# Layer-norm statistics of the one-head layers: combined on GpSimd in two parts of four chunks instead of one of eight

## The chip, the cores and the metric

The kernel runs on one core of a Trainium2 chip. The metric is the device time of one execution in microseconds (us), from the first to the last instruction; three executions of the kernel before lay between 2588.01 and 2589.99 us. Four engines compute: TensorE (PE in the profile, with its weight loads as PEld), VectorE (DVE), ScalarE (ACT) and GpSimd (POOL). SyncE (SP) issues the transfers.

## What is computed

The input `x` has 16 graphs of 1024 nodes with 256 features; `adj` is one 1024 x 1024 adjacency matrix for all. Four layers follow one another, and each one adds its result to `x`:

```python
h = jnp.maximum(_layernorm(x, axis=-1), 0.0)   # per node: (x - mean) / sqrt(var + 1e-5)
Wh = h @ W                                     # 256 x 256; 4 heads of 64, or 1 head of 256
e = leaky_relu(e_src[i] + e_dst[j])            # e_src, e_dst: Wh times two vectors
attn = softmax(where(adj, e, -inf), over j)
x = x + act(attn @ Wh)                         # elu in layers 0 to 2, relu in layer 3
```

Layers 0 and 2 have four heads, layers 1 and 3 have one. So there are 16 x 4 = 64 pairs of graph and layer, which the kernel calls steps: 32 of four heads and 32 of one.

## The kernel before

**Tiling.** A graph is held as `xs[b]`, 128 partitions x 8 chunks (`C`) x 256 features; `HALF` is four chunks. For one head, `weights` makes eight tiles of 128 x 1024 un-normalised attention weights on VectorE (`w`, line 347, in 18 buffers), and `aggregate` multiplies them with the projected features on TensorE (line 363). A step's aggregation is written as eight groups: in a four-head step four chunks of 128 nodes for one head, in a one-head step one chunk of nodes. Each group ends in a copy out of a PSUM bank by ScalarE (line 378).

**Order.** Four graphs are in flight (`STREAMS`), and the steps take turns among them, in the main alternating one four-head and one one-head step. The order of all instructions is written out by hand[...]. `preparation(n)` gives the pieces of work that step n needs before its aggregation, and each piece has a place in an agenda, counted in groups (8 to a step). Step n's preparation is spread over the aggregation of step n-2 and a little of n-1. For a one-head step the places are in `ONE`, from the start of step n-2:

```python
ONE = (2, 2, 2, 4, 4, 5, 5, 6, 6, 6, 6, 6, 6, 8, 8, 8, 8, 8, 10, 10, 12)
```

These are, in turn: the statistics of both halves (`stats(0)`, `stats(1)`) and their combination (`combine_all`) behind group 2; `normalise(0)` and `normalise(1)` behind group 4; the two transposes of half 0 behind group 5; the projection of half 0 (four chunks) and the two transposes of half 1 behind group 6; the rest later. The usual four-head step (`FOUR`) has its statistics eight groups before its start and its `combine_all` five before, so its combination comes behind group 3 of the same aggregation in which the next one-head step is prepared, and its `normalise(0)` behind group 5.

**The pieces around the change.**
- `finish` ends a step. Its `add(0)` and `add(1)` add the layer's result to `x`: one operation on VectorE (line 417), then one on GpSimd (line 418), for each half. After a four-head step they stand behind group 1 of the following aggregation, and the `stats` behind group 2 read the `x` that they wrote: a one-head layer of a graph follows its four-head layer at once.
- `stats` takes the eight chunks' statistics on VectorE (line 234), four chunks to a half.
- `combine` and `combine_end` turn them into a factor and a shift per node by ten operations, all on GpSimd for every step but the first: nine small ones, and a power (line 263).
- `normalise` applies them on ScalarE, one operation per chunk (line 275, tile `xn`).
- `transpose` turns four chunks on TensorE into a PSUM bank (line 283); ScalarE takes them out through a relu (line 284, tile `hT`).
- `project` multiplies a chunk with the layer's weights into a bank (line 294), and ScalarE copies it out (line 296, tile `whx`).

The banks are taken in turn by all of these from one pool of four, `ps`:

```python
ps = ctx.enter_context(tc.tile_pool(name="ps", bufs=4, space=PSUM))
```

Of the kernel before, what the change touches and what calls it, by code (L numbers as in the profile page):

```python
# [63 lines left out]
def kernel(ctx: ExitStack, tc: tile.TileContext, x, adj, ws, avs, out):  # L64
    nc = tc.nc
# [3 lines left out]
    HALF = C // 2  # L69
# [152 lines left out]
    def preparation(n):  # L222

        b, l = steps[n]
        H, slope, _, _ = LAYERS[l]
# [3 lines left out]
        def stats(half):  # L229
            if half == 0:  # L230
                st["bn"] = small.tile([P, C, 6], F32, name="bn")
            bn = st["bn"]
            for c in range(half * HALF, (half + 1) * HALF):
                nc.vector.bn_stats(bn[:, c, :], xs[b][:, c, :])  # L234
            if n == 0:
                q = slice(half * HALF, (half + 1) * HALF)
                if half == 1:
                    combine_end(slice(0, HALF), nc.vector)
                combine(q, nc.vector)
                if half == 1:  # L240
                    combine_end(q, nc.vector)

        def combine_all():
            if n > 0:
                combine(slice(0, C), nc.gpsimd)
                combine_end(slice(0, C), nc.gpsimd)

        def combine(q, engine):

            bn = st["bn"]  # L250
            m0, s0, m1, s1 = (bn[:, q, i] for i in (1, 2, 4, 5))
            if q.start == 0:
                st["rstd"] = small.tile([P, C], F32, name="rstd")
                st["shift"] = small.tile([P, C], F32, name="shift")
                st["dev"] = small.tile([P, C], F32, name="dev")
            rstd, shift, dev = (st[i][:, q] for i in ("rstd", "shift", "dev"))
            engine.tensor_tensor(dev, m0, m1, op=ALU.subtract)  # L257
            engine.tensor_tensor(dev, dev, dev, op=ALU.mult)
            engine.tensor_scalar(dev, dev, 0.25, EPS, op0=ALU.mult, op1=ALU.add)
            engine.tensor_tensor(rstd, s0, s1, op=ALU.add)  # L260
            engine.tensor_scalar(rstd, rstd, 1.0 / F, None, op0=ALU.mult)
            engine.tensor_tensor(rstd, rstd, dev, op=ALU.add)
            nc.gpsimd.tensor_tensor(rstd, rstd, neghalf[:, q], op=ALU.pow)  # L263
            engine.tensor_tensor(shift, m0, m1, op=ALU.add)  # L264

        def combine_end(q, engine):
            rstd, shift = (st[i][:, q] for i in ("rstd", "shift"))
            engine.tensor_tensor(shift, shift, rstd, op=ALU.mult)
            engine.tensor_scalar(shift, shift, -0.5, None, op0=ALU.mult)  # L269
# [45 lines left out]
        def rows():  # L315
# [6 lines left out]
            nc.sync.dma_start(out=st["grow"].rearrange("h c i -> c h i"), in_=gT)  # L322

        out = [lambda: stats(0), lambda: stats(1), combine_all, lambda: normalise(0), lambda: normalise(1)]
        for half in range(2):
            out += [lambda half=half, k=k: transpose(half, k) for k in range(K)]
# [130 lines left out]
    def plan(n):  # L457
        new = preparation(n)
        agenda.extend((at, n, piece, i == len(new) - 1) for i, (at, piece) in enumerate(new))
        agenda.sort(key=lambda a: a[:2])  # L460
# [52 lines left out]
    with tc.manual_schedule():  # L513
# [10 lines left out]
        nc.vector.tensor_copy(identb, ident)  # L524
        layer[0][1]()
        first = [piece for _, piece in preparation(0)]

        def sign(c):
# [98 lines left out]
```

## Time and profile before

| what | value |
|---|---|
| time, median of three | 2589.18 us |
| span of the profiled execution | 2586.6 us |
| granted TensorE clock, mean | 0.992 |
| busy: PE, PEld | 2508.0, 2257.8 us |
| busy: DVE, ACT, POOL | 2024.0, 1129.3, 1034.3 us |
| transfers | 128.98 MB, 50 GB/s on average |

A row of a group of instructions names the line, the engine, the operation and the tiles (written <- read), then the busy time, the mean of one in ns, and the idle time of the engine just before them with what ended it. A row of the timeline has the start in us, the length in us, the engine and the instructions, and in brackets the engine's idle time before them. The chain of waits is followed backwards from the last instruction: at each step to what released it, or to the instruction before it on its engine. Matmul ends are modelled, so a stretch in which PE counts as busy can hide a part of a wait; the starts of the weight loads (PEld) are then the better clock.

### The profile page before, as it was taken

How to read it: one execution, taken by the hardware profiler on the slowest of the kernel's cores; microseconds unless marked ns; L12 is line 12 of the kernel's file. 1: busy time of each engine (PE TensorE's matmuls, PEld its weight loads, DVE VectorE, ACT ScalarE, POOL GpSimd, SP SyncE). 2: the span in 40 equal slices, each digit the busy share in tenths (PEclk: the TensorE clock that was granted, in tenths of full speed). 3: DMA queues.
4: the chain of work that ended last, by engine and by line, in shares of the span. 5: the costliest groups of instructions: out<-in, count | busy, mean ns of one | idle time of the engine just before them, and what ended most of it. 6: DMA issues, size and time to landing. Idle time of an engine off the chain costs nothing.

```text
span 2586.6 us, 87821 instructions
## 1 busy us (share of the span) xinstructions
PE 2508.0 (97%) x40088; PEld 2257.8 (87%) x40088; DVE 2024.0 (78%) x2144; ACT 1129.3 (44%) x2502; POOL 1034.3 (40%) x1040
## 2 busy tenths in 40 slices
PE   6889999999999999999999999999999999999999
PEld 4788888899888899888899888998888998889888
DVE  5997678877778877778877778877778877787973
ACT  5344444434444444544344544344444345444341
POOL 2143444432443444543323444543433345444331
PEclk8899999999999999999999999999999999999999
DMA  3210011111112100102211111101112201111101
GB/s 142 73 44 35 18 34 43 43 60 59 59 51 76 43 27 27 43 35 75 76 53 66 43 35 43 43 19 68 50 59 76 76 11 43 35 43 43 52 18 57
DMA packets 36987, 128.98 MB, mean 50 GB/s; under 512 B 6278, under 2 KB 9094, under 8 KB 34696
## 3 DMA queue, kind: packets, MB, share of 16 engines
q1 hardware_dynamic: 36606, 123.36, 13.6%
q8 instruction: 314, 5.14, 0.8%
q14 instruction: 57, 0.47, 0.1%
q10 hardware_dynamic: 10, 0.00, 0.0%
HBM read 105.91 MB, written 17.43 MB: 48 GB/s over the span
## 4 chain that ended last, share of the span: by engine, by line
PE 57%; DVE 26%; POOL 9%; issue 5%; ACT 3%; DMA 1%; DVEq 0%; SPq 0%; ACTq 0%
PE bank L363 36%; DVE w L347 17%; PE bank L294 17%; POOL x L418 5%; PE bank L283 4%; DVE bn L234 3%; DVE e L417 2%; ACT xn L275 2%; DVE e L404 2%; POOL rstd L263 2%; DMA x<-in_x 0%; ACT e L411 0%; PE bank L318 0%; DVE r L395 0%; POOL shift L269 0%
## 5 line engine op out<-in xcount | busy, mean ns | idle before, releaser
L363 PE MATMUL bank<-whx,w 128*64 128x65 f32 x36864 | 1904.8, 241 | 32.6 <-DVE w L347 20.8
L363 PEld LDWEIGHTS bank<-whx,w 128*64 128x64 f32 x36864 | 1742.1, 144 | 176.5 <-DVE w L347 25.5
L347 DVE SCALAR_TENSOR_TENSOR w<-g,rcol,mask 128x1024 f32<-128x1024 f32 x1280 | 1540.4, 1273 | 378.0 <-PE bank L363 337.3
L378 ACT ACTIVATE y<-bank 128x260 f32<-128x260 f32 (+1 forms) x504 | 194.4, 386 | 1093.4 <-PE bank L363 1093.4
L306 POOL TENSOR_TENSOR whx<-whx 128x1024 f32<-128x1024 f32 x128 | 258.5, 2020 | 666.0 <-ACT whx L304 666.0
L405 POOL TENSOR_TENSOR y<-y,r 128x1024 f32<-128x1024 f32 x126 | 264.4, 2108 | 582.1 <-DVE e L404 454.9
L294 PE MATMUL bank<-wx,hT 128*128 128x264 f32 (+1 forms) x2048 | 476.5, 387 | 3.7 <-ACT hT L284 3.7
L294 PEld LDWEIGHTS bank<-wx,hT 128*128 128x128 f32 x2048 | 384.6, 191 | 66.3 <-ACT hT L284 4.6
L418 POOL TENSOR_TENSOR x<-x,e 128x1024 f32<-128x1024 f32 x96 | 248.0, 2593 | 135.7 <-DVE e L417 135.7
L275 ACT ACTIVATE xn<-x,shift,rstd 128x256 f32<-128x256 f32 x512 | 261.2, 590 | 82.9 <-POOL shift L269 80.8
L296 ACT ACTIVATE whx<-bank 128x264 f32<-128x264 f32 (+1 forms) x512 | 194.9, 386 | 208.1 <-PE bank L294 207.7
L234 DVE BATCH_NORM_STATS2 bn<-x 128x6 f32<-128x256 f32 x512 | 175.9, 412 | 97.2 <-POOL x L418 74.0
L417 DVE SCALAR_TENSOR_TENSOR e<-e,y 128x1024 f32<-128x1024 f32 x96 | 158.0, 1663 | 34.2 <-ACT e L411 26.9
L283 PE MATMUL bank<-ident,xn 128*128 128x128 f32 x1024 | 155.2, 281 | 22.9 <-ACT xn L275 22.4
L283 PEld LDWEIGHTS bank<-ident,xn 128*128 128x128 f32 x1024 | 120.4, 141 | 59.6 <-ACT xn L275 48.5
L342 ACT ACTIVATE g<-gs 128x1024 f32<-128x1024 f32 x160 | 163.6, 1022 | 11.1 <-DVE w L347 8.4
L284 ACT ACTIVATE hT<-bank 128x512 f32<-128x512 f32 x256 | 136.6, 585 | 0.3 <-PE bank L283 0.2
L263 POOL TENSOR_TENSOR rstd<-rstd,neghalf 128x8 f32<-128x8 f32 (+1 forms) x65 | 107.0, 1646 | 12.5 <-DVE shift L264 7.6
L411 ACT ACTIVATE e<-e 128x1024 f32<-128x1024 f32 x96 | 100.7, 1049 | 12.7 <-DVE e L404 12.7
L404 DVE SCALAR_TENSOR_TENSOR e<-y,r 128x1024 f32<-128x1024 f32 x64 | 75.6, 1222 | 2.5 <-DVE r L395 0.5
L420 DVE SCALAR_TENSOR_TENSOR x<-y,x 128x1024 f32<-128x1024 f32 x30 | 43.4, 1445 | 10.0 <-POOL y L405 10.0
L257 POOL TENSOR_TENSOR dev<-bn 128x8 f32<-128x8 f32 x63 | 14.6, 231 | 87.4 <-DVE bn L234 87.4
(63 smaller groups left out, 401.7 us busy)
## 6 DMA issues: line engine op xcount, KB each, us to landing
gs<-grow SPq DMA_DIRECT2D x160, 512.0 KB
x<-in_x SPq DMA_DIRECT2D x15, 1024.0 KB
out<-x SPq DMA_DIRECT2D x30, 512.0 KB
w<-in_adj SPq DMA_DIRECT2D x8, 512.0 KB
x<-in_x SPq DMA_DIRECT2D x2, 512.0 KB
wx<-in_L_gnn_W SPq DMA_DIRECT2D x8, 128.0 KB
out<-x SPq DMA_DIRECT2D x8, 128.0 KB
grow<-gT SPq DMA_DIRECT2D x32, 16.0 KB
```

What stands on the lines that cost most here:

```text
L234: nc.vector.bn_stats(bn[:, c, :], xs[b][:, c, :])
L275: nc.scalar.activation(xn[:, q, :], xs[b][:, c, :], AF.Identity, bias=st["shift"][:, c:c + 1], scale=st["rstd"][:, c:c + 1])
L283: nc.tensor.transpose(pt[:, q, :], st["xn", half][:, q, k * P:(k + 1) * P], ident)
L294: nc.tensor.matmul(pw, lhsT=st["hT", half][:, k, q * P:(q + 1) * P], rhs=wx[l][:, k, :], start=(k == 0), stop=(k == K - 1))
L296: nc.scalar.activation(st["whx"][:, c, :], pw, AF.Copy)
L306: nc.gpsimd.tensor_tensor(wh[:, :, :, 0:D], wh[:, :, :, 0:D], wh[:, :, :, D:D + 1].to_broadcast([P, HALF, H, D]), op=ALU.mult)
L347: nc.vector.scalar_tensor_tensor(w, state[n]["g", h], state[n]["rcol"][:, jc, h:h + 1], masks[LAYERS[steps[n][1]][3]][:, jc, :], op0=ALU.m ...
L363: nc.tensor.matmul(acc[o % P:o % P + cols, q, :], lhsT=st["w", h, jc][:, o:o + cols], rhs=st["whx"][:, jc, h * (D + 1):(h + 1) * (D + 1)], ...
L378: nc.scalar.activation(st["y"][:, i0:i0 + per, h, :], acc, AF.Copy)
L405: nc.gpsimd.tensor_tensor(yh, yh, rb, op=ALU.mult)
L417: nc.vector.scalar_tensor_tensor(e, e, -1.0, yh, op0=ALU.add, op1=ALU.max)
L418: nc.gpsimd.tensor_add(xh, xh, e)
```

## The change

In a one-head step, each half's statistics are combined on GpSimd at once behind their own `stats`, four chunks at a time, and `combine_all` is left to the four-head steps. It is for letting the first half's combination start before the second half's statistics are there, and for letting `normalise(0)` start before the second half is combined. The places in the agenda stay as they are.

```diff
             for c in range(half * HALF, (half + 1) * HALF):
                 nc.vector.bn_stats(bn[:, c, :], xs[b][:, c, :])
+            q = slice(half * HALF, (half + 1) * HALF)
             if n == 0:
-                q = slice(half * HALF, (half + 1) * HALF)
                 if half == 1:
                     combine_end(slice(0, HALF), nc.vector)
                 combine(q, nc.vector)
                 if half == 1:
                     combine_end(q, nc.vector)
+            elif H == 1:
+
+                combine(q, nc.gpsimd)
+                combine_end(q, nc.gpsimd)
 
         def combine_all():
-            if n > 0:
+            if n > 0 and H > 1:
                 combine(slice(0, C), nc.gpsimd)
                 combine_end(slice(0, C), nc.gpsimd)
```

## The prediction

> **What bounds the kernel now.** I read the page's busy shares first, then the groups by line with their waits, then the chain of waits in one round of the repeating pattern, and last the timelines of PEld, POOL and ACT around the place where the chain leaves GpSimd.
>
> The busy shares and two groups of the page:
>
> ```profile
> PE 2508.0 (97%) x40088; PEld 2257.8 (87%) x40088; DVE 2024.0 (78%) x2144; ACT 1129.3 (44%) x2502; POOL 1034.3 (40%) x1040
> ...
> L275 ACT ACTIVATE xn<-x,shift,rstd 128x256 f32<-128x256 f32 x512 | 261.2, 590 | 82.9 <-POOL shift L269 80.8
> ...
> L283 PEld LDWEIGHTS bank<-ident,xn 128*128 128x128 f32 x1024 | 120.4, 141 | 59.6 <-ACT xn L275 48.5
> ```
>
> TensorE is close to full. The largest wait of its weight loads is for `xn`, 48.5 us, and `xn` waits for the last operation of the combination. The rest of the question is how much of this is in one-head steps and on the path.
>
> The chain of waits between 1095 and 1180 us, one round of two steps (start, length, what):
>
> ```profile
> 1121.45 5.60 POOL x L418 x2
> ...
> 1128.56 0.22 POOL dev L257
> ...
> 1130.28 1.67 POOL rstd L263
> ...
> 1132.50 0.25 POOL shift L269
> 1132.75 0.02 issue
> 1132.78 2.08 ACT xn L275 x4
> 1134.86 0.04 issue
> 1134.90 0.77 PE bank L283 x5
> ```
>
> The chain comes from VectorE, passes the two adds of `finish`, the second half's statistics, the whole combination and four `xn`, and only then is on PE, where it stays until 1175.0. The weight loads there:
>
> ```profile
> 1115.92 17.24 PEld L363 LDWEIGHTS bank<-whx,w 128*128 128x128 f32 x80
> 1133.43 0.14 PEld L283 LDWEIGHTS bank<-ident,xn 128*128 128x128 f32 x1 [0.26 <-ACT xn L275]
> 1133.92 0.14 PEld L283 LDWEIGHTS bank<-ident,xn 128*128 128x128 f32 x1 [0.35 <-ACT xn L275]
> 1134.41 0.14 PEld L283 LDWEIGHTS bank<-ident,xn 128*128 128x128 f32 x1 [0.35 <-ACT xn L275]
> 1134.90 0.53 PEld L283 LDWEIGHTS bank<-ident,xn 128*128 128x128 f32 x5 [0.35 <-ACT xn L275]
> 1135.40 3.34 PEld L363 LDWEIGHTS bank<-whx,w 128*128 128x128 f32 x16
> 1138.77 3.46 PEld L294 LDWEIGHTS bank<-wx,hT 128*128 128x128 f32 x16
> 1142.26 1.01 PEld L283 LDWEIGHTS bank<-ident,xn 128*128 128x128 f32 x8
> 1143.24 0.74 PEld L363 LDWEIGHTS bank<-whx,w 128*128 128x128 f32 x4
> ```
>
> From 1133.17, when PEld is free, to 1135.40 are 2.23 us. The same eight transposes without a wait take 1.01 us (1142.23 to 1143.24). So this round loses 1.22 us. The wait list of PEld for 1095 to 1173 us has, beside these 1.3 us, only three waits of 0.2 to 0.3 us: nothing else holds TensorE up in a round. I went through all starts of line 283 in this way: from 432 to 2303 us there are 25 such places, about 78 us apart. In 24 of them the transposes are paced by `xn`; before the first of these the wait is 0 in three, 0.19 to 0.27 in thirteen, and 0.62 to 0.72 in eight. One (1290 us) loses only 0.35. Before 432 us the pattern is mostly VectorE's, and behind 2303 us there are small losses at 2359 and one at 2470, where the chain runs on through VectorE.
>
> [...] the combination takes 1128.56 to 1132.71, 4.15 us, when the next one follows at once. [...] the four-head step's combination stands ready from about 1119.3 us (its statistics end there) and starts at 1132.71, behind the other. [...] four `bn_stats` take 1.41 us both beside the second add (1124.76) and beside an idle GpSimd (1127.07). So I charge nothing for running small GpSimd operations beside them.
>
> **The change, part by part.**
>
> Removed: the wait of the first half for the second half's statistics. GpSimd is free at 1127.04, the first half's statistics are there at 1126.17, and the combination starts only at 1128.56. 1.5 us go.
>
> Cost of a part of four. The page groups kept apart by shape give:
>
> ```profile
> L263 POOL TENSOR_TENSOR rstd<-rstd,neghalf 128x8 f32<-128x8 f32 x63 | 105.0, 1666 | 4.9
> L263 POOL TENSOR_TENSOR rstd<-rstd,neghalf 128x4 f32<-128x4 f32 x2 | 2.0, 1024 | 7.6 <-DVE shift L264 7.6
> ```
>
> The power falls from 1.67 to 1.02 us. The nine small ones take about 0.2 us at eight columns; four columns are not in the trace on GpSimd, so between the same and, for scale, VectorE's 0.16. I keep them as they are: 4.15 - 0.64 = 3.51 us a part. Ends: if power and small ones had not shrunk at all, 4.15; if the small ones lost 0.04 each, 3.15.
>
> New times in this round, GpSimd: part one 1127.1 to 1130.6, part two (statistics there at 1128.5) to 1134.1, then the four-head step's combination, 4.15 us, to 1138.3. Before, it ended at 1136.88: it comes 1.4 us later. That is the cost, 2.9 us more of GpSimd in each one-head step (32 x 2.9 = 92 us of a 40% busy engine).
>
> New times, ACT: it is free at 1130.52. `xn` of half 0 from 1130.65 to 1132.7, all before TensorE comes at 1133.2. `xn` of half 1 waits for part two and starts at 1134.15; at the 0.49 us pitch of the trace four take 1.97 us, then the copy of group 5 at 1136.1 (before: 1136.72) and the two `hT` from 1136.4 to 1137.5 (before 1136.99). Queued behind half 1's wait are just these; the copy and `hT` get earlier all the same.
>
> TensorE: transposes at 1133.2, group 6 from 1134.2, projection from 1137.55, 1.22 us earlier, and `hT` is just there (first chunk 1137.0, second 1137.5). The whole wait is gone up to here.
>
> Then the moved combination bites. On ACT the four-head step's `normalise(0)` is next: it started at 1137.94 and now waits for 1138.3. Behind it are the copy of group 6 and those of the projection. Copy of group 6: start 1138.35 + 1.97 = 1140.3, end 1140.7 (before 1139.91, 1140.28). With four banks in turn (group 5, two transposes, group 6, then four chunks of the projection) the projection's fourth chunk needs exactly the bank of group 6. It started at 1138.98 + 3 x 0.87 = 1141.6; 1.22 us earlier is 1140.4; the bank is free at 1140.75. TensorE waits some 0.35 us, and 0.85 us stay. In the rounds with 0.72 us of first wait the transposes gain 1.68, but the bank is tied to GpSimd in the same way (add ends 1205.15, bank free at 1218.85, chunk before at 1219.7): 0.85 again. Where the first wait is 0, the gain of 0.96 is cut to 0.85 too.
>
> Does the gain last? From 1143 to 1175 the chain is on PE without a gap, and at 1175 the end of a group frees `w` buffers, which starts the VectorE chain that leads to the next adds. All of it moves with TensorE. VectorE's own order is unchanged, so the adds do not come later.
>
> Sum: 24 x 0.85 + 0.35 = 20.8 us; the small losses at 147, 273 and 2359 us (0.3 + 0.35 + 0.7) are on the path only in part, I take half, 0.7. Together 21.4 us: 2589.2 - 21.4 = 2567.8 us.
>
> **The rivals.**
> 1. The whole wait goes. If small operations shrink, or the fourth chunk doesn't wait for that bank, the gain is the loss itself: 24 x 0.96 + 8.8 (the sum of the first waits) + 0.4 + 0.7 = 33 us, 2556 us. For it: 0.04 us off each small operation would bring the four-head combination back by 0.7 us. Against it: operations of one column on GpSimd took 190 to 234 ns in this trace, so little depends on width.
> 2. Slower, by GpSimd's queue. If a part of four costs as much as eight (4.15 us), the three end at 1139.6, the copy of group 6 at 1142.0, and the fourth chunk starts 0.45 us later than before: 25 x 0.45 = 11 us, 2600 us. For it: 2.9 us already move a combination that ACT waits for in order. Against it: the power at four columns is in the trace, 1.02 us.
> 3. Slower, by the tracking of dependencies. If `xn` of half 0 waited for both parts, it would start at 1134.15, 1.4 us late: 25 x 1.4 = 35 us, 2624 us. Against it: in the first step, combined by halves already, `xn` starts at 9.23 us while the second power runs at 10.15.
> 4. No change: another chain of the same length takes over, VectorE's `w` for instance. Against it: every VectorE stretch in the round is released by TensorE. 2588 us.
>
> **How the numbers follow.** The forecast has 0.65, the first rival 0.19, the fourth 0.05, the second 0.08, the third 0.03. The predicted time is the forecast's, 2568 us. The range goes from the first rival's bound, 2555, to 2583, where a part costs 3.8 us, leaving 0.3 us a round. Faster by over 0.2% (5.2 us): 0.65 + 0.19 and a little of the uncertain sizes off, 0.83. Same 0.06, slower 0.11.
>
> **What would show it.** Right: the first `dev` (L257) of a round starts within 0.1 us of the end of the second add; the power appears 66 times at four columns, at 1.0 us, and 31 times at eight; the waits of L283 for `xn` fall from 48.5 us to about 10; a wait of L294 for ACT's copy appears at the fourth chunk, about 0.35 us in each round; rounds are 76.8 instead of 77.65 us. Wrong: `xn` of half 0 starting behind both parts; no bank wait at all (then rival 1); L283 waiting at the second half or at the four-head step.

## The result, and the profile after

The changed kernel takes 2569.4 us (median of four, 2568.6 to 2570.3), the kernel before 2588.6 us beside it: a ratio of 0.9927, with a 95% interval of 0.991 to 0.9944. That is 19 us, 0.7%. The forecast was 2568 us, a gain of 21.4 on the 2589.2 us from which it started. (Lines below `stats` have moved down by four: the transposes are L287, the projection L298, the aggregation L367, the copy of a group L382, the copy of `gT` L324.)

The rows of the page after the change that answer to those shown of before, with the one of the projection:

```profile
PE 2496.9 (97%) x40088; PEld 2258.1 (88%) x40088; DVE 2022.6 (79%) x2144; ACT 1129.5 (44%) x2502; POOL 1106.9 (43%) x1360
...
PE 85%; DVE 8%; ACT 3%; issue 2%; POOL 2%; DMA 1%; SPq 0%; DVEq 0%; POOLq 0%; ACTq 0%
...
L298 PEld LDWEIGHTS bank<-wx,hT 128*128 128x128 f32 x2048 | 382.3, 191 | 79.6 <-ACT y L382 14.9
...
L287 PEld LDWEIGHTS bank<-ident,xn 128*128 128x128 f32 x1024 | 120.0, 142 | 24.8 <-ACT xn L279 11.6
```

GpSimd is 73 us busier by its spans, and the kernel is faster. The transposes' wait for `xn` has fallen from 48.5 to 11.6 us. A wait of 14.9 us is new: the projection waits for the copy of a group out of its bank. The chain of waits was 57% on PE and 26% on DVE; it is now 85% and 8%.

The same place of a round as in the prediction, in the timeline of the changed kernel. GpSimd and ScalarE first:

```profile
1112.88 5.59 POOL L422 TENSOR_TENSOR x<-x,e 128x1024 f32<-128x1024 f32 x2 [1.16 <-DVE e L421]
...
1118.42 0.21 POOL L261 TENSOR_TENSOR dev<-bn 128x4 f32<-128x4 f32 x1
...
1121.99 2.08 ACT L279 ACTIVATE xn<-x,shift,rstd 128x256 f32<-128x256 f32 x4
...
1125.48 2.08 ACT L279 ACTIVATE xn<-x,shift,rstd 128x256 f32<-128x256 f32 x4 [1.41 <-POOL shift L273]
...
1129.65 2.07 ACT L279 ACTIVATE xn<-x,shift,rstd 128x256 f32<-128x256 f32 x4 [0.87 <-POOL shift L273]
1131.63 0.36 ACT L382 ACTIVATE y<-bank 128x257 f32<-128x257 f32 x1
```

The combination starts where the second add ends. The three lots of `xn` are those of the first half, of the second half, and of the four-head step; the last two wait for GpSimd. In the kernel before, the first lot began 5.74 us after the end of the second add (1127.04 to 1132.78); now it begins 3.5 us after it. Behind the third lot stands the copy of group 6. The weight loads of TensorE in that place:

```profile
1124.62 1.01 PEld L287 LDWEIGHTS bank<-ident,xn 128*128 128x128 f32 x8
1125.60 3.34 PEld L367 LDWEIGHTS bank<-whx,w 128*128 128x128 f32 x16
1128.97 2.58 PEld L298 LDWEIGHTS bank<-wx,hT 128*128 128x128 f32 x12
1132.05 0.73 PEld L298 LDWEIGHTS bank<-wx,hT 128*128 128x128 f32 x4 [0.49 <-ACT y L382]
```

The eight transposes run in one piece. Then come the projection's first three chunks, and the fourth waits for the copy.

The length of a round of two steps is taken on ScalarE, from one copy of `gT` of a four-head step to the next (`gT` is a small tile that every step writes once; it has 32 rows in a four-head step). First the kernel before, then the changed one:

```profile
1117.35 0.25 ACT L320 ACTIVATE gT<-bank 32x128 f32<-32x128 f32 x1
...
1194.99 0.25 ACT L320 ACTIVATE gT<-bank 32x128 f32<-32x128 f32 x1
```

```profile
1108.78 0.25 ACT L324 ACTIVATE gT<-bank 32x128 f32<-32x128 f32 x1
...
1185.55 0.25 ACT L324 ACTIVATE gT<-bank 32x128 f32<-32x128 f32 x1
```

The round here is 76.77 us, and 77.64 in the kernel before.

### The profile page after: what moved, and what is told of

Its sections match the earlier page's. It is cut to its first block, busy times and chain, and to the rows that moved or that the text cites. A ratio compares the mean times of both kernels' runs of the same rounds, so it can differ in the third digit from the quotient of the medians.

```text
span 2566.8 us, 88141 instructions
## 1 busy us (share of the span) xinstructions
PE 2496.9 (97%) x40088; PEld 2258.1 (88%) x40088; DVE 2022.6 (79%) x2144; ACT 1129.5 (44%) x2502; POOL 1106.9 (43%) x1360
## 4 chain that ended last, share of the span: by engine, by line
PE 85%; DVE 8%; ACT 3%; issue 2%; POOL 2%; DMA 1%; SPq 0%; DVEq 0%; POOLq 0%; ACTq 0%
PE bank L367 65%; PE bank L298 15%; DVE w L351 6%; PE bank L287 4%; ACT xn L279 2%; DVE bn L234 1%; DVE e L421 1%; POOL x L422 0%; POOL rstd L267 0%; DMA x<-in_x 0%; PE bank L322 0%; ACT y L382 0%; POOL shift L273 0%; DVE e L408 0%; DVE wx L156 0%
## 5 line engine op out<-in xcount | busy, mean ns | idle before, releaser
L367 PE MATMUL bank<-whx,w 128*64 128x65 f32 x36864 | 1907.9, 241 | 33.5 <-DVE w L351 21.8
L367 PEld LDWEIGHTS bank<-whx,w 128*64 128x64 f32 x36864 | 1745.0, 145 | 177.5 <-DVE w L351 26.4
L382 ACT ACTIVATE y<-bank 128x260 f32<-128x260 f32 (+1 forms) x504 | 194.2, 385 | 1094.8 <-PE bank L367 1094.8
L298 PE MATMUL bank<-wx,hT 128*128 128x264 f32 (+1 forms) x2048 | 481.9, 388 | 9.3 <-ACT y L382 4.6
L298 PEld LDWEIGHTS bank<-wx,hT 128*128 128x128 f32 x2048 | 382.3, 191 | 79.6 <-ACT y L382 14.9
L300 ACT ACTIVATE whx<-bank 128x264 f32<-128x264 f32 (+1 forms) x512 | 189.1, 385 | 184.4 <-PE bank L298 184.1
L287 PE MATMUL bank<-ident,xn 128*128 128x128 f32 x1024 | 137.2, 276 | 7.4 <-ACT xn L279 7.2
L287 PEld LDWEIGHTS bank<-ident,xn 128*128 128x128 f32 x1024 | 120.0, 142 | 24.8 <-ACT xn L279 11.6
L267 POOL TENSOR_TENSOR rstd<-rstd,neghalf 128x4 f32<-128x4 f32 (+1 forms) x97 | 120.2, 1239 | 15.0 <-DVE shift L268 7.6
L308 ACT ACTIVATE whx<-whx,nbias 128x16 f32<-128x16 f32 (+1 forms) x128 | 40.2, 314 | 4.2
```

Source lines behind the costliest of these rows:

```text
L287: nc.tensor.transpose(pt[:, q, :], st["xn", half][:, q, k * P:(k + 1) * P], ident)
L298: nc.tensor.matmul(pw, lhsT=st["hT", half][:, k, q * P:(q + 1) * P], rhs=wx[l][:, k, :], start=(k == 0), stop=(k == K - 1))
L300: nc.scalar.activation(st["whx"][:, c, :], pw, AF.Copy)
L367: nc.tensor.matmul(acc[o % P:o % P + cols, q, :], lhsT=st["w", h, jc][:, o:o + cols], rhs=st["whx"][:, jc, h * (D + 1):(h + 1) * (D + 1)], ...
L382: nc.scalar.activation(st["y"][:, i0:i0 + per, h, :], acc, AF.Copy)
```

## The experiments

Theory: each round gains what is left of its transposes' wait once the later four-head combination has taken its part through ScalarE's order and a PSUM bank. The runs of the first four kernels share one set of runs of the kernel before (2590.8 us), those of the last three another (2588.9 us). A run's own edit moves the line numbers further.

**One layer alone.** Only layer 1 is combined in parts:

```diff
-            elif H == 1:
+            elif l == 1:
...
-            if n > 0 and H > 1:
+            if n > 0 and l != 1:
```

> Only layer 1 is combined in two parts, layer 3 as before. Theory (each one-head round between 430 and 2310 us gives its 0.85 us by itself): about half of the 25 rounds are of layer 1, so half of the 19 us is gained, 2579 us, and the rounds of layer 1 last about 77 us, those of layer 3 about 78 us. Rival (the gain is one change of the whole pattern, or lies at the ends of the program): all of it or nothing, 2569 or 2589 us.

Measured: 2581.7 us, ratio 0.9966 (0.9953 to 0.9979), about 9 us. The projection waits 12 times for the copy, 7.6 us; in the changed kernel it is 24 times. The rounds come in runs of four, 77.19 / 77.18 / 76.72 / 76.72 us in one run and 77.63 / 77.64 in the next. The gain is made round by round: the rounds with a step of layer 1 have it, the others do not.

**The same instructions in another order.** The last two operations of part one stand behind part two's first eight:

```diff
             elif H == 1:
                 combine(q, nc.gpsimd)
-                combine_end(q, nc.gpsimd)
+                if half == 1:
+                    combine_end(slice(0, HALF), nc.gpsimd)
+                    combine_end(q, nc.gpsimd)
```

> The same GpSimd instructions as in the change, with the last two operations of the first part moved behind the second part's power and sum. The first part still starts as early, but its shift is complete only after part two's first eight operations. Theory (what pays is that xn of the first half starts while part two is still being combined): xn starts about 6.3 us after the end of the second add, 0.6 us later than in the kernel before, so slower than before by 0.4 to 0.7 us in each of 25 rounds, about 2600 us. Rival (starting the combination 1.5 us earlier is what pays): still faster than before, about 2570 us.

Measured: 2606.2 us, ratio 1.0058 (1.0041 to 1.0075). Most rounds are 78.18 and 78.64 us where the kernel before has 77.64 and 78.10, so 0.54 us longer, as expected. The total is 6 us above what was expected; two rounds are longer still (82.38 and 80.23 us, before 80.02 and 78.10), and what made them so is not shown. Its timeline:

```profile
1131.16 0.19 POOL L262 TENSOR_TENSOR dev<-bn 128x4 f32<-128x4 f32 x1
...
1137.20 0.23 POOL L274 TENSOR_SCALAR shift<-shift 128x4 f32<-128x4 f32 x1
...
1137.46 4.06 ACT L280 ACTIVATE xn<-x,shift,rstd 128x256 f32<-128x256 f32 x8 [2.78 <-POOL shift L274]
...
1138.11 0.14 PEld L288 LDWEIGHTS bank<-ident,xn 128*128 128x128 f32 x1 [0.79 <-ACT xn L280]
```

Part one starts as early as in the change, but `xn` starts 6.3 us after the add, and the transposes wait again, longer than in the kernel before. An early start is worth nothing by itself: what pays is when the first half's shift is complete.

**A later four-head combination, in both kernels.** Five small operations on a tile of their own stand ahead of it (the tile is made in lines not shown here):

```diff
+                if H > 1:
+                    for _ in range(5):
+                        nc.gpsimd.tensor_tensor(idle, idle, idle, op=ALU.mult)
                 combine(slice(0, C), nc.gpsimd)
```

In the kernel before:

> The kernel before, with five small GpSimd operations (128x8, about 1.4 us together) on a tile of their own ahead of every four-head combination. Theory (in the kernel before, the copy of group 6 behind xn has some 1.3 us of room before the fourth projection needs its bank): no change, 2586 to 2592 us, and no wait of the projection for that copy. Rival (any delay of the four-head combination costs its length): 32 x 1.4 us more, about 2630 us.

Measured: 2593.4 us, ratio 1.0008 (1.0002 to 1.0015), 2.5 us. That is just above the expected range, and far from the rival's 45 us. The five operations take 1.27 us there. The four-head `xn` starts 4.78 us after the first waiting transpose (1135.58 to 1140.36), where it was 4.51 us in the kernel before (1133.43 to 1137.94). Without the delay, GpSimd's shift was complete at 1136.88, and ScalarE was busy up to `hT` for another 1.06 us. These take up most of the delay, and the room at the bank is hardly drawn on. The projection does not wait:

```profile
1137.56 3.34 PEld L368 LDWEIGHTS bank<-whx,w 128*128 128x128 f32 x16
1140.93 3.46 PEld L299 LDWEIGHTS bank<-wx,hT 128*128 128x128 f32 x16
1144.42 1.01 PEld L288 LDWEIGHTS bank<-ident,xn 128*128 128x128 f32 x8
```

From the `gT` copy at 418.37 us to that at 2368.41 it takes 1950.0 us, as the kernel before does between the same two copies (416.30 to 2366.29). In the profiled executions the 2 us lie ahead of this stretch, so the rounds pay nothing.

In the changed kernel:

> The changed kernel with the same five small operations. Theory (there the four-head combination sets the end of each round, through ScalarE's order and the bank of group 6): 1.4 us more in each of 24 rounds, 34 us, about 2603 us, and the projection's waits for the copy grow from 14.9 to about 49 us. Rival (the bank wait is only where a slack of TensorE shows): same as the changed kernel, about 2570 us.

Measured: 2603.8 us, ratio 1.0053 (1.0038 to 1.0068); over the changed kernel's ratio that is 1.0053 / 0.9927 = 1.0127, 33 us. The rounds of 76.77 us in the changed kernel are 78.04 us here; the 1.27 us more are the length of what was put in. From its list of waits for PEld (us in total, times, longest):

```profile
PEld bank L303 <- ACT y L387: 46.2, 25, 2.2
```

So in the rounds the same delay is free in one kernel and is paid in full in the other.

**The four-head normalisations one group later, with the change.** The fourth and fifth numbers are the places of `normalise(0)` and `normalise(1)`, counted in groups from the step's start:

```diff
-FOUR = (-8, -8, -5, -3, -2, -1, -1, 0, 0, 0, 0, 0, 0, 2, 2, 2, 2, 3, 8, 8, 10)
+FOUR = (-8, -8, -5, -2, -1, -1, -1, 0, 0, 0, 0, 0, 0, 2, 2, 2, 2, 3, 8, 8, 10)
```

> The changed kernel with the four-head step's two normalisations one group later (places -2 and -1 in place of -3 and -2), so that the copies of group 6 and of the projection no longer stand behind them on ScalarE. TensorE's and GpSimd's orders are the same. Theory (the remaining wait is for the bank that this order holds back): the 14.9 us of waits of the projection for the copy go, the rounds fall to about 76.2 us, 2555 us. Rival (the four-head transposes or hT then come late and take it back): 2565 us or more, with waits of the transposes for xn.

Measured: 2559.4 us, ratio 0.9883 (0.987 to 0.9897); against the changed kernel 0.9883 / 0.9927 = 0.9956, 11 us. In the wait list the projection's wait for the copy is gone, and the transposes do not wait in the rounds either (11.8 us in all, at the same places as in the changed kernel). The rounds are 76.42 us, nearly all of them alike. Its weight loads:

```profile
1122.32 1.01 PEld L287 LDWEIGHTS bank<-ident,xn 128*128 128x128 f32 x8
1123.30 3.34 PEld L367 LDWEIGHTS bank<-whx,w 128*128 128x128 f32 x16
1126.67 3.46 PEld L298 LDWEIGHTS bank<-wx,hT 128*128 128x128 f32 x16
1130.15 1.01 PEld L287 LDWEIGHTS bank<-ident,xn 128*128 128x128 f32 x8
1131.13 3.34 PEld L367 LDWEIGHTS bank<-whx,w 128*128 128x128 f32 x16
```

The mechanism was right and the size too large: removing 14.9 us of waits gained 11. The wait of the weight loads contains a gap that stands there without it too. The four chunks of the projection took 4.00 us on PE with the wait (at 1129.18 in the changed kernel) and 3.65 without (at 1138.98 in the kernel before), so 0.35 of the 0.49 us is loss, and such rounds shrink by just this (76.77 to 76.42). Rounds with a wait of some 0.95 us shrink by 0.81 (77.23 to 76.42).

**Both normalisations behind group 6, with the change** (-2 and -2 in `FOUR`):

> As the one before, with both four-head normalisations behind group 6 (places -2 and -2). Theory: the same gain, 2555 us, if the copy of group 7 behind eight xn is not needed soon; it comes some 1.5 us later than in the other order, so at most some us worse.

Measured: 2558.2 us, ratio 0.9882 (0.9867 to 0.9897): not to be told from the one before. Both orders beat both kernels.

**The same places without the change:**

> The kernel before with the same places -2 and -1 and no splitting. Theory (before, the copies behind the four-head normalisation were in time, and the loss is at the one-head transposes): no change, 2586 to 2591 us. Rival (the order on ScalarE costs both kernels): faster by about as much as it makes the changed kernel faster, 2575 us.

Measured: 2589.3 us, ratio 1.0003 (0.9995 to 1.0011). No difference, as the theory has it. Its transposes wait 48.0 us for `xn`, as before. The order on ScalarE cost nothing until the four-head combination came later.

## Why the prediction was right

**The wait at the transposes.** It was to go in all rounds and the sum to fall to about 10 us: 11.6 us are left, none of them at one of the 25 places that were counted. What is left is at the start and at 274 and 2338 us.

**A part of four.** The prediction worked out 3.51 us, and 1118.42 to 1121.93 is 3.51 us. The groups of the page, kept apart by shape, have the power at four columns 66 times, and a small operation as long as at eight columns, as was assumed:

```profile
L267 POOL TENSOR_TENSOR rstd<-rstd,neghalf 128x4 f32<-128x4 f32 x66 | 68.5, 1038 | 12.6 <-DVE shift L268 7.6
L262 POOL TENSOR_TENSOR dev<-dev 128x4 f32<-128x4 f32 x64 | 12.9, 201 | 5.0
L262 POOL TENSOR_TENSOR dev<-dev 128x8 f32<-128x8 f32 x31 | 6.3, 203 | 2.4
```

This refutes the second rival, which needed a part as long as the whole, and one of the two ways of the first, smaller small operations. Its other way, no wait for the bank, is refuted by the new wait. The third needed `xn` of the first half to wait for both parts: it starts at 1121.99, while part two runs from 1121.93 to 1125.41. The fourth, no change, is refuted by the time.

**The cost.** The four-head combination was to come later and to hold the copy of group 6 until the fourth chunk needs its bank. That is the new wait, in 24 rounds. Where it is 0.49 us, 0.35 of it is loss, as was forecast for each round. The two delays show that 1.27 us were free before, and nothing after. With the later places the wait is gone, and in the round at 1100 us the chain of waits is on PE alone.

**The sum.** 0.85 us a round was forecast, 0.87 us is measured in most rounds (77.64 to 76.77, 78.10 to 77.23). Over the 25 rounds between the same two `gT` copies the kernel before takes 1950.0 us and the changed one 1928.2 us (416.00 to 2344.18): 21.8 us, where 20.8 were forecast. About half of the difference is the round with the place at 1290 us, which became 0.90 us shorter (80.02 to 79.12) and not 0.35.

**What was missed.** Of the small losses at 147, 273 and 2359 us, 0.7 us were to be gained. Only the first wait is gone, and the changed kernel is 0.3 us ahead at the copy at 416 us; the other two waits stand as they were.

From the last of these copies to the end the changed kernel takes 222.6 us in its profiled execution, the kernel before 220.3: 2.3 us are lost again there, for which the forecast had no term. GpSimd is not the cause. A table of two stretches of four-head aggregation there, first in the changed kernel and then the same two in the kernel before (stretch, its length, busy time of PE, PEld, DVE, ACT and POOL, granted clock, busy share of the DMA engines, GB/s):

```profile
2426.00:2435.30 9.30, 9.17 (x256) 9.11 (x256) 6.72 (x4) 4.26 (x11) 8.64 (x4) 0.82 0.02 4
2443.00:2451.20 8.20, 8.20 (x228) 8.20 (x228) 8.20 (x13) 2.35 (x5) 5.64 (x20) 0.79 0.02 4
```

```profile
2448.20:2455.70 7.50, 7.48 (x256) 7.48 (x256) 6.48 (x5) 4.15 (x10) 7.50 (x4) 1.00 0.02 4
2462.70:2469.40 6.70, 6.70 (x228) 6.70 (x228) 6.70 (x12) 0.39 (x1) 3.42 (x10) 1.00 0.02 5
```

The same 256 and 228 weight loads take 1.6 and 1.5 us more, at a granted clock of 0.82 and 0.79 instead of 1.00. From one `gT` copy to the next, 1.6 us of the first come through to the end (54.62 to 56.18 us) and 0.8 us of the second (44.60 to 45.37).

No instruction of the split is the cause either. The kernel with only layer 1 in parts has, from the same copy on, the same instructions as the kernel before on every engine, and it too takes 222.6 us there; the two intervals between `gT` copies are 55.86 and 45.69 us in it. So the split's own work does not explain these 2.3 us; the last section has the granted clock there. That the forecast came within 2 us of the time is in part luck, since errors of both signs met in it: the rounds gave 1.0 us more than forecast, and the start and the end gave less.

## What to carry to other kernels

When a bound engine waits for a chain on another, ask when the chain's first usable piece is complete, and split there; starting early is worth nothing by itself. Then follow what the split pushes back on the engines behind it, where work written later stands behind work that waits: here a step that could be 1.27 us late for free lost this room, and 11 us of possible gain with it, beside the 19 us made, until the order on ScalarE was changed. The same reordering did nothing in the old kernel and was worth 11 us in the new one, so a reordering is worth trying again after each change.

## What the runs showed of the hardware

The nine small GpSimd operations of a combination cost nearly the same at four columns as at eight (1.92 and 2.01 us together, by their mean spans in the changed kernel). The power took longer with more columns: 1038 ns at four, 1668 at eight, 0.16 us a column between them. (One with a single column, line 170, takes 0.71 us, more than that slope would give.) So cutting the combination in two adds 2.9 us: two parts of 3.51 in place of one of 4.15.

ScalarE took its work in the order written, also where a later piece was ready first. In the changed kernel the weight loads of group 6 end at 1128.94 us, and the copy of the group starts at 1131.63, 2.69 us later, behind the third lot of `xn`, which waited for GpSimd until 1129.65. With the two normalisations written one group later, the loads end at 1126.64 and the copy starts at 1127.08, 0.44 us later.

The granted clock at the end of the changed kernel is 0.50 in one part of each of the two stretches: from 2426.14 to 2429.54 us and from 2443.21 to 2446.60, 3.4 us each. It is 1.00 between them (2429.60 to 2443.10) and behind them (2446.70 to 2451.20). At half the clock 3.4 us hold the work of 1.7, an estimate from these two figures; the loads took 1.6 and 1.5 us longer. Nearer the start both kernels have such a part: the clock is 0.50 from 279.20 to 282.50 us in the changed kernel, and from 279.80 to 283.10 in the kernel before.

Just ahead of the first of the two, the weight loads of the changed kernel wait for ScalarE from 2422.76 to 2426.12 us, and PE is busy for 0.41 us of these 3.36. The kernel before has the same wait of 3.36 us, from 2444.86 to 2448.22, with PE busy for the same 0.41 us; there the clock stays at 1.00, in the wait and from 2448.30 to 2469.40 behind it. So a wait of this length was followed by half speed in one execution and not in the other. What decides it is not shown, and no run moved the wait on purpose.

Over all nine profiles, the two intervals between `gT` copies in which these stretches lie take 54.62 and 44.6 us in the three kernels without the split, and 55.86 to 56.19 and 45.35 to 46.74 in the six with it, the one with only layer 1 in parts among them. Each is a single execution. The mean granted clock of one and the same kernel differs from execution to execution: over 24 of the kernel before it lay between 0.990 and 0.993.
